# Sums of weights on VectorE behind the first operand sums, two transfer queues, and second-pass sums beside the last pair of the first pass

## The chip, the cores and the metric

One core of one Trainium2 chip runs the whole program in one launch. The metric is the device time in microseconds (us), given as the median over executions; every execution whose state is on record was in the undisturbed state ("fast", which means not more than 1.5% above the fastest of the same kernel), save one single look whose state can't be told. "Window" rows and "order of time" rows below count from the start of the profiled execution.

## The reference, cut to what matters

Two graph layers over 128 graphs of 64 nodes with 768 features, each behind a layer norm and a ReLU:

```python
h = jnp.maximum(_layernorm(x), 0.0)
x = x + layer0(h, adj, ...)    # three 768x768 products (Wadj, Wrev, Wself), two of them averaged
                               # over neighbours, and a relation table looked up by the entry of adj
h = jnp.maximum(_layernorm(x), 0.0)
x = x + layer1(h, adj, ...)    # six attention heads and a gate: two 768x768 products
```

The kernel makes one pass over all tiles for layer 0, then one for layer 1. A step of a pass handles two tiles of 128 rows, "a pair". The big products are computed blockwise with seven block products in place of eight; that needs four sums of weight blocks, called T1 to T4, and sums of the operands (S1 to S4). For layer 0 a sum of weights is three VectorE or GpSimd instructions (three matrices), for layer 1 two.

Of the kernel before, what the change touches and what calls it, by code (L numbers as in the profile page):

```python
# [8 lines left out]
F32 = mybir.dt.float32  # L9
# [6 lines left out]
P = 128  # L16
# [6 lines left out]
def kernel(  # L23
# [48 lines left out]
    nc = tc.nc  # L72
    G, N, D = x.shape
    NREL = e_t.shape[1]
# [9 lines left out]
    HALF = D // 2  # L84
# [25 lines left out]
    def row(v, parts):  # L110

        n = 1
        for s in v.shape:
            n *= s
        return bass.AP(tensor=v.tensor, offset=v.offset, ap=[[0, parts], [1, n]])
# [21 lines left out]
    for g in range(GT):  # L137
        s = slice(g * N, (g + 1) * N)
# [2 lines left out]
    mhalf = const.tile([P, 1], F32, name="mhalf")  # L141
    nc.vector.memset(mhalf, -0.5)

    def stats(src, to):

        st = small.tile([P, 2, 6], F32, name="st")
        for i in range(2):
            nc.vector.bn_stats(st[:, i, :], src[:, i * HALF : (i + 1) * HALF])
        mv = small.tile([P, 2], F32, name="mv")
        nc.vector.bn_aggr(mv, st.rearrange("p a b -> p (a b)"))  # L150
        ve = small.tile([P, 1], F32, name="ve")
        nc.vector.tensor_scalar(ve, mv[:, 1:2], EPS, None, op0=OP.add)
        nc.gpsimd.tensor_tensor(to[:, 0:1], ve, mhalf, op=OP.pow)
        nc.vector.scalar_tensor_tensor(to[:, 1:2], mv[:, 0:1], -1.0, to[:, 0:1],
                                       op0=OP.mult, op1=OP.mult)
# [3 lines left out]
    def block(name, mats, place):  # L159
        return [keep.tile([P, KH, HALF], F32, name=f"{name}{s}", tag=f"w{place}{s}") if s < 2 else  # L160
                keep.tile([P, KH, HALF], F32, name=f"{name}{s}", tag="wl", bufs=7)
                for s in range(mats)]

    def sums_of_weights(w, mats):


        for eng, to, a, b in ((nc.vector, "T1", "T3", "11"), (nc.vector, "T2", "22", "T1"),
                              (nc.gpsimd, "T3", "22", "T3"), (nc.vector, "T4", "21", "T2")):
            for s in range(mats):
                tc.keep_in_program_order(eng.tensor_sub(w[to][s], w[a][s], w[b][s]))  # L170


    bv, H1 = {}, {}

    def load_h(p):
        for k in range(2):
            t = 2 * p + k
            H1[t] = keep.tile([P, D], F32, name="h1", tag="x", bufs=8)
            nc.sync.dma_start(H1[t], H1D[p][k * P : (k + 1) * P, :])

    def fetch():

        def blk_of(name, place, h, q):
            bv[name] = block(f"bv{name}", 2, place)
            for s, src in enumerate((w_cat, hw_t)):
                nc.sync.dma_start(
                    bv[name][s],
                    src[h * HALF : (h + 1) * HALF, q * HALF : (q + 1) * HALF].rearrange(
                        "(k p) n -> p k n", p=P))

        def own(name, place):
            bv[name] = block(f"bv{name}", 2, place)

        return [(4, lambda: load_h(0)),
                (9, lambda: blk_of("11", "11", 0, 0)),
                (19, lambda: blk_of("21", "21", 1, 0)),
                (28, lambda: blk_of("T3", "T1", 0, 1)),
                (37, lambda: blk_of("22", "T2", 1, 1)),
                (47, lambda: own("T1", "T4")),
                (58, lambda: own("T2", "T3"))]  # L200


    with ExitStack() as px:
        wa = px.enter_context(tc.tile_pool(name="wa", bufs=1))
        work = px.enter_context(tc.tile_pool(name="work0", bufs=2))
# [3 lines left out]
        X, AI = {}, {}  # L209

        def load(p):
            if p >= NP:
                return
            AI[p] = work.tile([P, 2, 2, N], I32, name="ai")
            for d, src in ((0, adj), (1, adj_t)):
                nc.sync.dma_start(
                    AI[p][:, :, d, :],
                    src[p * 2 * GT : (p + 1) * 2 * GT].rearrange("(t g) i j -> (g i) t j", g=GT))
            for t in (2 * p, 2 * p + 1):
                X[t] = keep.tile([P, D], F32, name="x", bufs=8)  # L220
                nc.sync.dma_start(X[t], xf[t * P : (t + 1) * P, :])

        load(0)


        bw = {n: block(f"bw{n}", 3, n) for n in ("11", "21", "22", "T1", "T2", "T3", "T4")}

        def load_block(to, h, q):
            for s, src in enumerate((wadj_t, wrev_t, wself_t)):
                nc.sync.dma_start(  # L230
                    to[s], src.rearrange("(k h p) n -> h p k n", h=2, p=P)[h][:, :, q * HALF : (q + 1) * HALF])

        load_block(bw["11"], 0, 0)
        load_block(bw["21"], 1, 0)
        load_block(bw["T3"], 0, 1)
        load_block(bw["22"], 1, 1)
        et = wa.tile([P, NREL], F32, name="et")
        nc.sync.dma_start(et, e_t)
        wrt = work.tile([P, 2, D], F32, name="wrt", tag="a1")
        nc.sync.dma_start(wrt[:, 0, :], wr_t)  # L240
        nc.sync.dma_start(wrt[:, 1, :], wrr_t)

        bia = work.tile([5, D], F32, name="bia", tag="s3")
        for i, v in enumerate((br, brr, badj, brev, bself)):
            nc.sync.dma_start(bia[i : i + 1, :], row(v, 1))
        load(1)

        identb = wa.tile([P, P], BF16, name="identb")
        nc.vector.tensor_copy(identb, ident)
        blkb = wa.tile([P, P], BF16, name="blkb")  # L250
# [56 lines left out]

        def norm(t):
            to = small.tile([P, 2], F32, name="rn")
            stats(X[t], to)  # L310
            h = H0[t] = work.tile([P, D], F32, name="h0")
            nc.scalar.activation(h, X[t], AF.Relu, scale=to[:, 0:1], bias=to[:, 1:2])

        def prep(p):

            af = ADF[p] = work.tile([P, 2, 2, N], F32, name="af", bufs=1)
            nc.vector.tensor_copy(af, AI[p])
            ab = AB[p] = work.tile([P, 2, 2, N], BF16, name="ab", bufs=1)
            nc.vector.tensor_copy(ab, af)

# [33 lines left out]
        def count(p, k):  # L354

            eq = work.tile([P, 2, NG, N], BF16, name="eq", bufs=1)
            nc.vector.tensor_tensor(
                eq, GR[p][:, k, :, None, :].to_broadcast([P, 2, NG, N]),
                vals[:, None, :, :].to_broadcast([P, 2, NG, N]), op=OP.is_equal)
            nc.vector.tensor_tensor(  # L360
                eq, eq, WO[p][:, k, :, None, :].to_broadcast([P, 2, NG, N]), op=OP.mult)
            nc.vector.tensor_reduce(SUM[p][:, k], eq, AX.X, OP.add)
# [58 lines left out]
        def sum2(p):  # L421
            S2[p] = work.tile([P, KH, 3, P], F32, name="s2", bufs=1)
            for q in range(KH):
                nc.gpsimd.tensor_sub(S2[p][:, q], S1[p][:, q], A1[p][:, q, 0])  # L424

        def sum4(p):
            S4[p] = work.tile([P, KH, 3, P], F32, name="s4", bufs=1)
            for q in range(KH):
                nc.gpsimd.tensor_sub(S4[p][:, q], A1[p][:, q, 1], S2[p][:, q])
# [65 lines left out]
        def finish(p):  # L495
            for k in range(2):
                t = 2 * p + k
                to = small.tile([P, 2], F32, name="rn")
                stats(X[t], to)
                h = keep.tile([P, D], F32, name="hf", bufs=2)  # L500
                nc.scalar.activation(h, X[t], AF.Relu, scale=to[:, 0:1], bias=to[:, 1:2])
                nc.sync.dma_start(H1D[p][k * P : (k + 1) * P, :], h)
                nc.gpsimd.tensor_add(X[t], X[t], h)
                nc.sync.dma_start(XH1[p][k * P : (k + 1) * P, :], X[t])
# [23 lines left out]


        prep(0)  # L530
        norm(0)
        norm(1)
        prep_r(0)
# [1 line left out]
            for q in range(KH):  # L535
                operands(0, k, q)
        sum2(0)
        sums_of_weights(bw, 3)
        sum4(0)
        prep_c(0)  # L540
        late = [(14, build_table), (15, lambda: count(0, 0)),
# [9 lines left out]
    with ExitStack() as px:  # L551
        wb = px.enter_context(tc.tile_pool(name="wb", bufs=1))
        work = px.enter_context(tc.tile_pool(name="work1", bufs=2))
# [3 lines left out]
        XH, AI = {}, {}  # L557
# [231 lines left out]
        def before(p):  # L789

            if p >= NP:
                return []
            return [(0, lambda: load(p + 1)),
                    (11, lambda: turn(p, 0, 0)),
                    (14, lambda: turn(p, 0, 1)),
                    (17, lambda: turn(p, 1, 1)),
                    (20, lambda: turn(p, 1, 0))]
# [48 lines left out]
                steps.append((99, lambda q=q: final(t1, q * HALF, (q + 1) * HALF)))  # L846
            return steps

        bv["T4"] = block("bvT4", 2, "22")
        sums_of_weights(bv, 2)  # L850
        for _, step in before(0):
            step()
        for p in range(NP):
            more = [(3, lambda: finish(NP - 1))] if p == 0 else []
            if p == NP - 1:
                more += last()
            merged(main(p), before(p + 1) + behind(p - 1) + more)
# [45 lines left out]
```

## The kernel before: what the change touches

The sums of weights, T3 on GpSimd, all pinned in program order:

```python
def sums_of_weights(w, mats):
    for eng, to, a, b in ((nc.vector, "T1", "T3", "11"), (nc.vector, "T2", "22", "T1"),
                          (nc.gpsimd, "T3", "22", "T3"), (nc.vector, "T4", "21", "T2")):
        for s in range(mats):
            tc.keep_in_program_order(eng.tensor_sub(w[to][s], w[a][s], w[b][s]))
```

`keep_in_program_order` pins an instruction behind all that was written down before it for its engine; everything else may be moved by the scheduler. The transfers, all on one queue, in this order:

```python
load(0)                            # first pair: adjacency and x
load_block(bw["11"], 0, 0)         # four weight blocks, 1.77 MB each
load_block(bw["21"], 1, 0)
load_block(bw["T3"], 0, 1)
load_block(bw["22"], 1, 1)
nc.sync.dma_start(et, e_t)         # 40 KB, needed early by VectorE (es <- et, ids)
nc.sync.dma_start(wrt[:, 0, :], wr_t)
nc.sync.dma_start(wrt[:, 1, :], wrr_t)
# [cut: five bias rows]
load(1)                            # second pair
```

The opening of the first pass, and the start of the second:

```python
prep(0); norm(0); norm(1); prep_r(0)
for k in range(2):
    for q in range(KH):
        operands(0, k, q)          # first operand sums, from PSUM
sum2(0)
sums_of_weights(bw, 3)
sum4(0)
# [cut]
bv["T4"] = block("bvT4", 2, "22")  # second pass
sums_of_weights(bv, 2)
for _, step in before(0):
    step()                         # its first operand sums s3 and s1
```

## Time and profile before

| kernel before | us |
|---|---|
| median of three executions | 2695.43 (2694.94 to 2698.22) |
| profiled execution, first to last instruction (2700.46 as timed) | 2698.6 |
| TensorE busy / idle in it | 2628.7 / 69.9 |
| hole 1, wait for the first operand sums | 9.92, up to 27.95 |
| hole 2, wait for the second pair's converted adjacency | 8.08, up to 53.16 |
| hole 3, join of the passes, wait for `s1` | 8.97, up to 1587.29 |

TensorE is the engine that sets the time, so the table is read from its idle time: a change of order that shortens neither a hole nor the half clock behind one can't shorten the kernel. The prediction shows the lines themselves. A row in the order of time reads: start, length, engine and source line, operation, output<-input, shapes, number of instructions, and in brackets how long the engine stood before it and what released it.

### The profile page before, as it was taken

To read this page: it belongs to the slowest core of one execution; us is meant where nothing else is said; L and a number is where in the kernel's file an instruction comes from. 1 tells how busy PE (TensorE), PEld (TensorE's weight loads), DVE (VectorE), ACT (ScalarE), POOL (GpSimd) and SP (SyncE) were. 2 spreads that over 40 slices of the span, in tenths; PEclk is the share of its full clock that TensorE was granted. 3 is DMA by queue.
4 is the path that set the end of the run, shared out by engine and by line. 5 is a ranking of instruction groups with operands and counts; after the bars stand their busy time and mean duration, and the time that the engine had idled before them with its cause. 6 is when DMAs were issued, how large, how long until landed. Compare 5 with 4: busy or idle time off the path is not lost.

```text
span 2698.6 us, 29601 instructions
## 1 busy us (share of the span) xinstructions
PE 2628.7 (97%) x10348; PEld 1608.9 (60%) x10348; DVE 1814.8 (67%) x4235; ACT 843.3 (31%) x1892; POOL 632.1 (23%) x662
## 2 busy tenths in 40 slices
PE   5999999999999999999999989999999999999997
PEld 3556666565666656566665556666666666666664
DVE  6956465565646556564655258888888888888888
ACT  1212111121211112111111025555555555555555
POOL 3322232312223231222322231111111111111111
PEclk7999999999999999999999999999999999999998
DMA  5112121111212112121211322222222222222211
GB/s 172 45 38 74 38 75 37 53 60 38 74 38 75 38 45 67 37 75 38 74 37 42 135 79 73 72 66 68 69 70 73 73 68 67 70 69 73 73 60 47
DMA packets 91211, 173.47 MB, mean 64 GB/s; under 512 B 32958, under 2 KB 41521, under 8 KB 91062
## 3 DMA queue, kind: packets, MB, share of 16 engines
q1 hardware_dynamic: 91062, 171.58, 19.3%
q8 instruction: 82, 1.34, 0.2%
q14 instruction: 67, 0.55, 0.1%
HBM read 95.67 MB, written 75.50 MB: 63 GB/s over the span
## 4 chain that ended last, share of the span: by engine, by line
PE 71%; DVE 19%; ACT 6%; issue 3%; SPq 1%; DMA 1%; POOL 0%; ACTq 0%; DVEq 0%
PE pwa L443 20%; PE pwb L443 14%; PE pwd L443 7%; PE pwc L443 7%; PE pb L399 5%; PE pma L631 5%; PE pmc L631 5%; DVE no L712 4%; PE pmb L631 3%; DVE f L783 2%; ACT e L782 2%; DVE f L784 2%; DVE f L785 2%; DVE f L773 2%; PE ps L768 2%
## 5 line engine op out<-in xcount | busy, mean ns | idle before, releaser
L443 PE MATMUL pwa<-bwT,s 128*128 128x384 f32 x1152 | 391.2, 489 | 0.5 <-DVE x L460 0.5
L443 PEld LDWEIGHTS pwa<-bwT,s 128*128 128x128 f32 x1152 | 215.0, 190 | 145.6 <-issue 8.5
L631 PE MATMUL pma<-bvT,s 128*128 128x384 f32 x768 | 289.1, 487 | 0.0
L424 POOL TENSOR_TENSOR s<-s,a 128x384 f32<-128x384 f32 x96 | 94.8, 1014 | 633.1 <-PE pwa L443 596.7
L719 POOL TENSOR_TENSOR pr<-th,wsd 128x768 f32<-128x768 f32 x64 | 137.1, 2143 | 424.6 <-ACT th L708 217.5
L460 DVE TENSOR_TENSOR x<-pwa,x 128x384 f32<-128x384 f32 x128 | 69.5, 543 | 210.8 <-PE pwa L443 179.4
L443 PE MATMUL pwb<-bw,s 128*128 128x384 f32 x576 | 201.6, 489 | 0.0
L443 PE MATMUL pwb<-bwT,s 128*128 128x384 f32 x576 | 201.3, 495 | 0.0
L443 PE MATMUL pwa<-bw,a 128*128 128x384 f32 x576 | 197.5, 492 | 2.8 <-DVE x L460 2.8
L443 PE MATMUL pwd<-bwT,a 128*128 128x384 f32 x576 | 191.3, 486 | 0.0
L443 PE MATMUL pwc<-bw,a 128*128 128x384 f32 x576 | 191.0, 486 | 0.0
L411 ACT COPY a<-pb 128x768 f32<-128x768 f32 x96 | 73.7, 801 | 373.2 <-PE pb L399 373.2
L388 ACT COPY cntT<-pb 117x128 bf16<-117x128 bf16 (+1 forms) x128 | 27.8, 269 | 482.9 <-PE pb L386 482.9
L399 PE MATMUL pb<-r,h 64*128 64x192 f32 x1536 | 153.7, 339 | 18.2 <-DVE s L419 11.0
L399 PEld LDWEIGHTS pb<-r,h 64*128 64x128 f32 x1536 | 124.4, 189 | 73.6 <-issue 62.3
L717 ACT ACTIVATE dg<-idc,sd 128x64 f32<-128x64 f32 x384 | 128.5, 345 | 123.7 <-DVE no L712 123.5
L631 PEld LDWEIGHTS pma<-bvT,s 128*128 128x128 f32 x768 | 131.8, 191 | 53.3 <-issue 0.8
L712 DVE SCALAR_TENSOR_TENSOR no<-th,wsd 128x128 f32<-128x128 f32 x384 | 152.0, 396 | 5.5 <-ACT th L708 0.9
L631 PE MATMUL pmb<-bvT,s 128*128 128x384 f32 x384 | 146.6, 492 | 9.0 <-DVE s L616 9.0
L443 PEld LDWEIGHTS pwc<-bw,a 128*128 128x128 f32 x576 | 109.4, 190 | 76.3
L443 PEld LDWEIGHTS pwd<-bwT,a 128*128 128x128 f32 x576 | 109.4, 190 | 76.3 <-issue 0.2
L443 PEld LDWEIGHTS pwa<-bw,a 128*128 128x128 f32 x576 | 107.5, 192 | 73.7 <-issue 9.8
(141 smaller groups left out, 4618.0 us busy)
## 6 DMA issues: line engine op xcount, KB each, us to landing
x<-in_x_dram SPq DMA_DIRECT2D x64, 384.0 KB
h<-hf SPq DMA_DIRECT2D x64, 384.0 KB
xh<-x SPq DMA_DIRECT2D x64, 384.0 KB
h<-h SPq DMA_DIRECT2D x64, 384.0 KB
x<-xh SPq DMA_DIRECT2D x64, 384.0 KB
out_dram<-f SPq DMA_DIRECT2D x62, 384.0 KB
ai<-in_adj_dram SPq DMA_DIRECT2D x64, 64.0 KB
ai<-in_adj_t_dram SPq DMA_DIRECT2D x32, 64.0 KB
```

The source lines that it names most:

```text
L399: nc.tensor.matmul(ps[:, g, i * 3 * N : (i + 1) * 3 * N], H0[t][s, kb * P : (kb + 1) * P], rts[p % 2][s, k].rearrange("p s n -> p (s n)"), ...
L411: nc.scalar.copy(A1[p][:, q].rearrange("p h s (g n) -> p g (h s) n", g=GT), pv)
L424: nc.gpsimd.tensor_sub(S2[p][:, q], S1[p][:, q], A1[p][:, q, 0])
L443: nc.tensor.matmul(bank[b][:, :HALF], a()[:, q, s, :], bw[w][s][:, q, :], start=(first and q == s == 0), stop=(q == KH - 1 and s == 2), sk ...
L460: nc.vector.tensor_add(v, bank[b][:, :HALF], v)
L631: nc.tensor.matmul(bank[b, s][:, :HALF], a[p][:, q, :], bv[w][s][:, q, :], start=(first and q == 0), stop=(q == KH - 1), skip_group_check= ...
L712: nc.vector.scalar_tensor_tensor(no, th[:, h, :], 1.0, wsd[:, 1, h * DO : (h + 1) * DO], op0=OP.mult, op1=OP.mult, accum_out=sd[:, 1, h : ...
L717: nc.scalar.activation(dg[:, h, :], idc, AF.Copy, scale=sd[:, 1, h : h + 1])
L719: nc.gpsimd.tensor_mul(pr, th, wsd[:, 0, :].rearrange("p (h o) -> p h o", h=H))
L768: nc.tensor.matmul(po[:, i, :], PT[t][:, h, :], HS[t][:, h, :], start=True, stop=True)
L773: nc.vector.scalar_tensor_tensor(FF[t][:, h * DO : (h + 1) * DO], po[:, i, :DO], ri[:, i, :], bb, op0=OP.mult, op1=OP.add)
L782: nc.scalar.activation(e, f, AF.Exp, bias=mone)
```

## The change

The intent: no wait for a transfer on VectorE's path in the opening, no GpSimd sum beside VectorE's, and no sums left between the passes. Cut to its core:

```diff
-    def sums_of_weights(w, mats):                       # T3 on GpSimd
+    SUMS = {"T1": ("T3", "11"), "T2": ("22", "T1"), "T4": ("21", "T2"), "T3": ("22", "T3")}
+    def sum_of_weights(w, to, behind=False):            # all on VectorE
+        a, b = SUMS[to]
+        for s, t in enumerate(w[to]):
+            ins = nc.vector.tensor_sub(t, w[a][s], w[b][s])
+            if behind: tc.keep_in_program_order(ins)
     def stats(src, to, behind=False):
         for i in range(2):
-            nc.vector.bn_stats(st[:, i, :], ...)
+            ins = nc.vector.bn_stats(st[:, i, :], ...)
+            if behind and i == 0:                       # third pair's tiles only
+                tc.keep_in_program_order(ins)
         load(0)
+        nc.scalar.dma_start(et, e_t)                    # and the five bias rows
         load_block(bw["11"], 0, 0)
+        load(1)
         load_block(bw["21"], 1, 0)                      # T3, 22 as before
-        nc.sync.dma_start(et, e_t)
         # [cut: wrt as before; bias rows and load(1) no longer here]
# pins on the third pair's conversion and on counts of the first two pairs: [cut]
-        sums_of_weights(bw, 3)
+        for to in SUMS:
+            sum_of_weights(bw, to, behind=True)
# second pass: in the last pair of the first
-   (47, lambda: own("T1", "T4")),
-   (58, lambda: own("T2", "T3"))
+   (47, lambda: (own("T1", "T4"), sum_of_weights(bv, "T1"), sum_of_weights(bv, "T3"))),
+   (58, lambda: (own("T2", "T3"), sum_of_weights(bv, "T2")))
-        bv["T4"] = block("bvT4", 2, "22")
-        sums_of_weights(bv, 2)
         for _, step in before(0): step()
+        bv["T4"] = block("bvT4", 2, "22")
+        sum_of_weights(bv, "T4")
```

More of the change, by code (lines that the diff above doesn't have):

```diff
@@ L142, with stats @@
     nc.vector.memset(mhalf, -0.5)
-    def stats(src, to):
+    def stats(src, to, behind=False):
         st = small.tile([P, 2, 6], F32, name="st")
         for i in range(2):
-            nc.vector.bn_stats(st[:, i, :], src[:, i * HALF : (i + 1) * HALF])
+            ins = nc.vector.bn_stats(st[:, i, :], src[:, i * HALF : (i + 1) * HALF])
+            if behind and i == 0:
+                tc.keep_in_program_order(ins)
         mv = small.tile([P, 2], F32, name="mv")
@@ L162, in block @@
                 for s in range(mats)]
-    def sums_of_weights(w, mats):
-        for eng, to, a, b in ((nc.vector, "T1", "T3", "11"), (nc.vector, "T2", "22", "T1"),
-                              (nc.gpsimd, "T3", "22", "T3"), (nc.vector, "T4", "21", "T2")):
-            for s in range(mats):
-                tc.keep_in_program_order(eng.tensor_sub(w[to][s], w[a][s], w[b][s]))
+    SUMS = {"T1": ("T3", "11"), "T2": ("22", "T1"), "T4": ("21", "T2"), "T3": ("22", "T3")}
[3 more added lines that the diff above has]
+            ins = nc.vector.tensor_sub(t, w[a][s], w[b][s])
+            if behind:
+                tc.keep_in_program_order(ins)
     bv, H1 = {}, {}
@@ L198, in fetch @@
                 (37, lambda: blk_of("22", "T2", 1, 1)),
-                (47, lambda: own("T1", "T4")),
-                (58, lambda: own("T2", "T3"))]
+                (47, lambda: (own("T1", "T4"), sum_of_weights(bv, "T1"), sum_of_weights(bv, "T3"))),
+                (58, lambda: (own("T2", "T3"), sum_of_weights(bv, "T2")))]
     with ExitStack() as px:
@@ L223 @@
         load(0)
+        et = wa.tile([P, NREL], F32, name="et")
+        nc.scalar.dma_start(et, e_t)
+        bia = work.tile([5, D], F32, name="bia", tag="s3")
+        for i, v in enumerate((br, brr, badj, brev, bself)):
+            nc.scalar.dma_start(bia[i : i + 1, :], row(v, 1))
         bw = {n: block(f"bw{n}", 3, n) for n in ("11", "21", "22", "T1", "T2", "T3", "T4")}
@@ L236 @@
         load_block(bw["22"], 1, 1)
-        et = wa.tile([P, NREL], F32, name="et")
-        nc.sync.dma_start(et, e_t)
         wrt = work.tile([P, 2, D], F32, name="wrt", tag="a1")
@@ L241 @@
         nc.sync.dma_start(wrt[:, 1, :], wrr_t)
-        bia = work.tile([5, D], F32, name="bia", tag="s3")
-        for i, v in enumerate((br, brr, badj, brev, bself)):
-            nc.sync.dma_start(bia[i : i + 1, :], row(v, 1))
-        load(1)
         identb = wa.tile([P, P], BF16, name="identb")
@@ L309, in norm @@
             to = small.tile([P, 2], F32, name="rn")
-            stats(X[t], to)
+            stats(X[t], to, behind=(t // 2 == 2))
             h = H0[t] = work.tile([P, D], F32, name="h0")
@@ L316, in prep @@
             af = ADF[p] = work.tile([P, 2, 2, N], F32, name="af", bufs=1)
-            nc.vector.tensor_copy(af, AI[p])
+            ins = nc.vector.tensor_copy(af, AI[p])
+            if p == 2:
+                tc.keep_in_program_order(ins)
             ab = AB[p] = work.tile([P, 2, 2, N], BF16, name="ab", bufs=1)
@@ L356, in count @@
             eq = work.tile([P, 2, NG, N], BF16, name="eq", bufs=1)
-            nc.vector.tensor_tensor(
+            ins = nc.vector.tensor_tensor(
                 eq, GR[p][:, k, :, None, :].to_broadcast([P, 2, NG, N]),
                 vals[:, None, :, :].to_broadcast([P, 2, NG, N]), op=OP.is_equal)
+            if p < 2 and k == 0:
+                tc.keep_in_program_order(ins)
             nc.vector.tensor_tensor(
```

## The prediction

> **What bounds the kernel now.** I read the page's busy shares first, then a table of busy time by stretch, then the order of time in the two stretches that stand out, and last every instruction of the line that forms the sums of weights.
>
> ```profile
> PE 2628.7 (97%) x10348; PEld 1608.9 (60%) x10348; DVE 1814.8 (67%) x4235; ACT 843.3 (31%) x1892; POOL 632.1 (23%) x662
> ```
>
> TensorE is busy for 2628.7 of 2698.6 us, so only 69.9 us of idle time exist for any reordering to win back, plus what a lowered clock costs behind such a gap. The stretches show where they lie (columns: stretch, its length, busy time of each engine, granted clock, DMA share, GB/s):
>
> ```profile
> 0.00:10.00 10.00, 0.37 (x1) 0.10 (x1) 6.97 (x24) 1.28 (x1) 2.93 (x14) 1.00 0.76 247
> 10.00:20.00 10.00, 6.25 (x42) 4.84 (x42) 2.43 (x16) 5.28 (x7) 0.55 (x1) 1.00 1.06 377
> 20.00:30.00 10.00, 2.06 (x9) 1.65 (x10) 2.17 (x6) 0.37 (x1) 1.97 (x3) 0.58 0.83 282
> 40.00:50.00 10.00, 5.08 (x16) 2.66 (x14) 10.00 (x4) 0.00 (x0) 8.48 (x3) 0.94 0.00 0
> 50.00:60.00 10.00, 6.84 (x11) 2.18 (x11) 9.80 (x26) 2.05 (x2) 1.10 (x2) 0.50 0.06 13
> 60.00:70.00 10.00, 10.00 (x29) 4.87 (x30) 4.94 (x10) 1.59 (x2) 0.00 (x0) 0.70 0.00 0
> 1570.00:1580.00 10.00, 8.32 (x33) 4.68 (x31) 9.73 (x7) 3.44 (x6) 7.91 (x4) 1.00 0.94 330
> 1580.00:1590.00 10.00, 2.71 (x4) 1.51 (x5) 9.83 (x12) 0.00 (x0) 5.38 (x4) 0.57 0.38 144
> ```
>
> Three holes matter: 18 to 28 us, 45 to 53 us, 1578 to 1587 us. The rest of the idle time is the first 11.65 us (loads and first operands), 2.8 us at 100 to 102.65, and some 17 us in the drain from 2650 on; the change touches neither the first nor the last. In order of time:
>
> ```profile
> 26.56 0.31 DVE L273 TENSOR_TENSOR es<-et,ids 128x39 f32<-128x39 f32 x2 [13.60 <-DMA et<-in_e_t_dram]
> 27.95 1.65 PE L399 MATMUL pb<-r,h 64*128 64x192 f32 x8 [9.92 <-DVE s L419]
> 31.08 5.49 DVE L170 TENSOR_TENSOR bwT<-bwT,bw 128x1152 f32<-128x1152 f32 x3
> 36.49 15.75 DVE L170 TENSOR_TENSOR bwT<-bw,bwT 128x1152 f32<-128x1152 f32 x6
> 53.16 0.39 PE L347 MATMUL pb<-ab,blkb 128*128 128x256 bf16 x1 [8.08 <-DVE ab L319]
> 61.81 4.86 PE L443 MATMUL pwb<-bwT,s 128*128 128x384 f32 x8
> 102.65 7.77 PE L443 MATMUL pwa<-bw,a 128*128 128x384 f32 x18 [2.79 <-DVE x L460]
> 1587.29 4.21 PE L631 MATMUL pmb<-bvT,s 128*128 128x384 f32 x6 [8.97 <-DVE s L616]
> ```
>
> The first hole is VectorE standing for 13.60 us on `et`, a 40 KB table queued behind 8.0 MB; TensorE's operands wait behind it (9.92). The second: TensorE's in-order list reaches the second pair's row sums, whose input VectorE converts only after nine sums (31.08 to 52.24). The third: the same sums for the second pass, with TensorE needing the `s1` that follows them (8.97). The sums are slow because GpSimd forms T3 at the same time (duration in ns, least/median/most):
>
> ```profile
> L170 DVE TENSOR_TENSOR bwT<-bw,bwT x6: 1344/2951/3771, 36.5 to 50.9; 128x1152 f32<-128x1152 f32 x6
> L170 POOL TENSOR_TENSOR bwT<-bw,bwT x3: 3722/3732/3735, 37.4 to 44.8; 128x1152 f32<-128x1152 f32 x3
> ```
>
> **What the Trainium skill says.** (1) "GPSIMD Engine Reference", section 8, Key points: GpSimd shares its SBUF interfaces with VectorE and collides with VectorE instructions that have two SBUF inputs. The trace agrees: one sum takes 1.344 us alone and 3.771 us beside GpSimd's. (2) "TensorE: Matmul & The Clock Gate", Part 1: after an idle window of about 3.4 us the array runs at half clock, and needs about as long a busy one to recover. It agrees: after the 8.08 us gap the granted clock is 0.50, and 8 matmul instructions take 4.86 us against some 2.6 warm (18 take 5.8). (3) The same page, "Engine queue depths": VectorE is strictly first in, first out; the 13.60 us wait that held ready work shows it. (4) "DMA: Bandwidth & Descriptors", "Issuing engines are not separate DMA queues": transfers from several engines interleave on the same 16 DMA engines. A second queue therefore adds no bandwidth; it lets the small tables pass the big weights. The share of 1.06 at 377 GB/s says that bandwidth is the limit until 28 us.
>
> **The change part by part.** The built order of instructions says more than the diff: from the third pair to the end of the first pass, and in the second pass after its first pair, it is the same on every engine. So the 47.36 us of a pair stay, and only the opening and the join of the passes can move.
>
> *Transfers.* `et` and the five bias rows go to ScalarE's queue and land in the first few us: VectorE's 13.60 us wait goes. The second pair's load moves up behind the first weights (0.92 MB, about 2.4 us at 385 GB/s), landing near 13.5 us instead of 34.4.
>
> *VectorE's opening.* In the built order the second pair's conversion and statistics now stand before the first operand sums: about 20 instructions, 5.5 us from 13.3, with one wait on GpSimd's power: to 18.7. The first operand sums come at 18.8 to 19.9 (26.8 to 27.7 before); TensorE resumes at 20 after 2 us of idling, perhaps still warm, and runs to about 24 to 27. Then I see a flaw: only the first of two statistics instructions of a tile is pinned behind the sums. The second half of the third pair's first tile stands between the first and second operand sums. Its data come after all the weights, the second pair, 0.79 MB of relation weights and 0.13 MB of adjacency: `et` landed at 26.5 behind 8.0 MB; now 2.2 MB more stand ahead of or in it, 2.2/0.385 = 5.8 us, so 32.3 us. The operand sums then end at 34.7, not the 31.2 of before.
>
> *The twelve sums.* GpSimd's operand sums collide with the first three as before: 5.5 us. Nine more alone at 1.27 us from start to start (1.344 with its overlap): 11.4. 34.7 + 16.9 = 51.6 us, against 52.24 before without T3. As VectorE work this is even; what changes is what stands behind.
>
> *TensorE.* From the second operand sum at 33.9: row sums 0.4, three matmuls of two instructions cold at 1.3 = 3.9, five warm 3.2, the relation table 5.5 (8.7 cold before, about 4.4 warm), four 2.6, nine with T1 5.8: 55.3. The next operands need a reciprocal behind the sums, 51.6 + 3.9 of VectorE work = 55.5. From there a pair's rest at full clock: three blocks of 18 at 5.8 each and the last block 5.8 = 23.2, operand products 48 instructions 4.6, transposes and counts 2.8: 30.6, and 2 us of small waits: 88.1. VectorE's own remaining list of about 24 us ends near 80 to 83, because the third pair's preparation and counts are pinned away. So the second pair starts at 88 instead of 102.65, 14.5 earlier, and without the cold restart (7.77 against 5.8 for its first 18 instructions) another 1.9: 16.4. I take off 2.4 for a clock that may fall through the table's narrow matmuls and for waits at the end of the pair: 14.
>
> *The join of the passes.* T1 starts when the last pair's T4 matmuls are done (about 1553.5) and T3 follows, their transfers having stopped at 1553; T2 starts when T3's old block is free (about 1560). That is six sums, 8 us, in a stretch where VectorE is nearly empty. T4's two start at 1565.5 and end at 1568. Then `s3` and `s1` at 1569.5 to 1570.6, and TensorE needs `s1` at about 1572.9, so no wait: 8.97 us gone, plus half of the 4.21 us cold stretch, 2.1. One risk is an addition into x that now stands behind T2 and must free a bank before 1563.4: it comes at 1562.5. I take 10.5 of 11.1.
>
> Sum: 2695.4 - 14 - 10.5 = 2671 us.
>
> **The rivals.** *A: the misplaced statistics cancel the opening's gain.* TensorE idles from about 26 to 34 and is cold again; if the table stays cold (+4) and VectorE's counts still end last (the chain of waits before goes through them between 67 and 102), the opening gives 5 to 8: about 2678. For it: the hole only moves. Against it: the 8 us gap at 45 and its 13 us of half clock have no cause left. *B: the load is hidden and the opening as the author meant it.* If the third pair's tile lands by 26, the sums end near 44 and the opening gives 22: about 2662. Against it: 1.06 of DMA share. *C: the join stalls anew.* If the late addition or the old blocks hold a sum, TensorE waits 2 to 5 us and the clock may drop: 2675. *D: the second pass takes the gain back.* VectorE is at 80% there, but TensorE is at 99% (39.7 of 40 us), so an earlier start should reach the end whole.
>
> **Range and chances.** The opening alone spreads from 6 to 22, the join from 6 to 11.5, and the day's runs spread by 3.3 us: 2662 to 2681. Over 2% would need 54 us, nearly all idle time there is; over 2% slower would need something that no step here makes. So 0.01 faster, 0.985 same, 0.005 slower.
>
> **What would show it.** VectorE's wait on `et` gone; a wait of about 11 us on the transfer of x ahead of a statistics instruction, ending near 32; L173 sums of 1.34 us with none on GpSimd; the first matmul of the second pair (18 instructions into `pwa`) near 88; in the join no TensorE gap over 1 us and a granted clock of 1.00 from 1540 on. I am wrong if the sums stay near 2.5 us beside an idle GpSimd, if TensorE idles over 4 us between 34 and 88, if the join keeps a wait on `s1`, or if the distance between two pairs leaves 47.4.

## The result, and the profile after

The changed kernel takes 2676.58 us (2676.50 to 2677.65, 4 executions) against 2696.82 us (2694.94 to 2700.03, 4 executions) of the kernel before beside it: ratio 0.9925, 95% interval 0.9907 to 0.9942, so faster, but by less than 2%. Ratios here are the mean time of one kernel's fast executions over that of the other's of the same rounds, so not quite the ratio of the medians quoted. By medians 20.2 us are gained, where 24.4 (2695.43 to 2671) were predicted.

The busy line of the changed kernel's page:

```profile
PE 2620.3 (98%) x10348; PEld 1607.3 (60%) x10348; DVE 1810.1 (68%) x4240; ACT 843.2 (32%) x1892; POOL 612.6 (23%) x657
```

TensorE's idle time fell from 69.9 to 54.4 us, and its busy time by 8.4 us with the same 10348 instructions; the mean granted clock rose from 0.990 to 0.995, so less of it ran at half clock. The second queue moves 0.06 MB. By stretch, as before:

```profile
20.00:30.00 10.00, 4.34 (x18) 2.47 (x18) 0.49 (x2) 1.40 (x2) 2.00 (x2) 0.91 1.07 372
30.00:40.00 10.00, 6.19 (x13) 3.53 (x14) 7.73 (x8) 0.00 (x0) 5.95 (x4) 0.57 0.47 156
40.00:50.00 10.00, 10.00 (x30) 4.71 (x29) 10.00 (x9) 0.00 (x0) 1.09 (x1) 1.00 0.00 0
100.00:110.00 10.00, 9.20 (x50) 5.79 (x50) 10.00 (x17) 4.15 (x6) 5.57 (x4) 1.00 0.47 165
1570.00:1580.00 10.00, 10.00 (x34) 6.03 (x33) 3.63 (x7) 0.48 (x1) 1.99 (x2) 1.00 0.32 119
```

The first hole is still there, moved to 25 to 34 us: VectorE is busy for 0.49 us of 20 to 30, while transfers run at 372 GB/s. The second hole is gone (40 to 50: TensorE 10.00 at clock 1.00), the third too (1570 to 1580). VectorE has no idle time left at 100 to 110 (it was busy for 9.64 of 10 before). VectorE's work in order of time, the three rows that set the opening:

```profile
32.27 0.56 DVE L148 BATCH_NORM_STATS2 st<-x 128x6 f32<-128x384 f32 x1 [11.78 <-DMA x<-in_x_dram]
34.59 5.65 DVE L173 TENSOR_TENSOR bwT<-bwT,bw 128x1152 f32<-128x1152 f32 x3
40.16 12.29 DVE L173 TENSOR_TENSOR bwT<-bw,bwT 128x1152 f32<-128x1152 f32 x9
```

The wait for `et` is gone, and in its place VectorE stands 11.78 us on the transfer of a tile of x: the half of the third pair's statistics that the change did not pin, with operand sums behind it. The nine sums without a GpSimd partner take 12.29 us, 1.37 each. TensorE's rows (`pb<-r,h` are operand products; `pwa`, `pwb`, `pwc` the main accumulations; `wrt,es` the relation table):

```profile
20.64 0.92 PE L407 MATMUL pb<-r,h 64*128 64x192 f32 x8 [1.36 <-DVE s L427]
33.81 0.40 PE L353 MATMUL pb<-ab,blkb 128*128 128x256 bf16 x1 [8.83 <-DVE s L427]
34.00 4.05 PE L451 MATMUL pwa<-bw,a 128*128 128x384 f32 x6
41.41 1.45 PE L295 MATMUL pb<-wrt,es 128*81 128x384 f32 x4
56.25 0.92 PE L407 MATMUL pb<-r,h 64*128 64x192 f32 x8 [1.76 <-DVE r L358]
89.86 4.03 PE L451 MATMUL pwa<-bw,a 128*128 128x384 f32 x12
102.55 1.57 PE L407 MATMUL pb<-r,h 64*128 64x192 f32 x16 [0.80 <-DVE r L358]
1559.98 2.10 PE L641 MATMUL pmb<-bvT,s 128*128 128x384 f32 x6
```

Before, the matmuls behind the second hole ran at half clock to about 66 us. Now the clock is half at 34 us (six instructions in 4.05 us, which take 2.10 warm) and back by 41.4 (four table instructions in 1.45 us, 2.77 in the profile before). The second pair starts at 89.86 instead of 102.65, without a cold restart. The last row is the first use of the second pass's T1: no wait, full clock, where it was 4.21 us behind a wait of 8.97.

From the third pair's second block to the last pair's fourth, the two traces run in step: 157.61 to 1548.59 before, 144.84 to 1535.82 after, 1390.98 us in both. The two ends are where the time moved: 12.8 us in the opening, and 11.6 in the join (a later product of the second pass, 1603.09 before, 1578.72 after: 24.4 in all).

### The profile page after: what moved, and what is told of

It reads as the page before. It is cut to its first block, busy times and chain, and to the rows that moved or that the text cites. A ratio compares the mean times of both kernels' runs of the same rounds, so it can differ in the third digit from the quotient of the medians.

```text
span 2674.7 us, 29599 instructions
## 1 busy us (share of the span) xinstructions
PE 2620.3 (98%) x10348; PEld 1607.3 (60%) x10348; DVE 1810.1 (68%) x4240; ACT 843.2 (32%) x1892; POOL 612.6 (23%) x657
## 3 DMA queue, kind: packets, MB, share of 16 engines
q8 instruction: 82, 1.34, 0.2%
## 4 chain that ended last, share of the span: by engine, by line
PE 71%; DVE 19%; ACT 6%; issue 3%; DMA 1%; SPq 0%; POOL 0%; ACTq 0%; DVEq 0%
PE pwa L451 20%; PE pwb L451 14%; PE pwd L451 7%; PE pwc L451 7%; PE pma L641 5%; PE pb L407 5%; PE pmc L641 5%; DVE no L722 4%; PE pmb L641 3%; DVE f L793 2%; ACT e L792 2%; DVE f L794 2%; DVE f L795 2%; DVE f L783 2%; PE ps L778 2%
## 5 line engine op out<-in xcount | busy, mean ns | idle before, releaser
L451 PEld LDWEIGHTS pwb<-bwT,s 128*128 128x128 f32 x576 | 106.2, 190 | 69.0 <-issue 6.7
```

Source lines behind the costliest of these rows:

```text
L451: nc.tensor.matmul(bank[b][:, :HALF], a()[:, q, s, :], bw[w][s][:, q, :], start=(first and q == s == 0), stop=(q == KH - 1 and s == 2), sk ...
```

## The experiments

Each kernel was correct. "Beside" means in the same rounds on the same chip. The changed kernel ran again beside experiments 2 and 3 only. Where experiments 5, 7, 8 and 9 are set against it, or against `pin_both`, the runs are of other rounds, those of 7, 8 and 9 also of other chips; the kernel before had medians of 2695.89 to 2698.91 in the four sets of rounds, so a difference of some 3 us between sets needs a trace to back it.

### 1. The changed kernel once more (`after_again`)

No edit; a check of the result in other rounds.

> The changed kernel once more, as a yardstick on the same chip as the next three. Expected 2676.6 us, within 1.5, and again a wait of VectorE of about 11.8 us on the transfer of x ahead of a statistics instruction, ending near 32.3 us.

Measured: 2676.78 us (2676.65 to 2678.61, 4 executions), ratio to the kernel before 0.9923 (0.9909 to 0.9936). The kernel before, beside it, had 2698.91 us and spread over 2694.42 to 2700.33. VectorE's wait on x was there again (11.65 us, up to 32.37). The changed kernel repeats within about 2 us, the kernel before only within 6; that spread comes up again in experiment 6.

### 2. Both halves of the statistics pinned (`pin_both`)

```diff
-            if behind and i == 0:
+            if behind:
```

In the built order a single VectorE instruction moves: the second half of the third pair's first statistics, from between the operand sums to behind the twelve sums.

> One instruction moves: the second statistics instruction of the third pair's first tile goes behind the sums of weights too. My theory: its 11.8 us wait holds the second and third operand sums and with them everything on VectorE, so without it the operand sums end near 23 us, the twelve sums wait for the last weights (landing near 29 us) and end near 43 instead of 52.4; TensorE is then held by the relation table's transfers until about 35 us. About 8 us less than the changed kernel: 2668, between 2665 and 2671. Rival: the wait only covers another one (weights and the table come at the same time, or VectorE's list behind the sums ends last whatever stands ahead), then 2674 to 2677.

Measured: 2668.14 us (2667.55 to 2670.24, 4 executions), ratio 0.9888 (0.9873 to 0.9903), beside the changed kernel's 2676.78: another 8.6 us for one condition. VectorE's sums, then two TensorE rows:

```profile
23.45 5.99 DVE L173 TENSOR_TENSOR bwT<-bwT,bw 128x1152 f32<-128x1152 f32 x3
29.36 12.29 DVE L173 TENSOR_TENSOR bwT<-bw,bwT 128x1152 f32<-128x1152 f32 x9
```

```profile
33.91 0.84 PE L297 MATMUL pb<-bia,eb 5*81 5x384 f32 x2 [1.97 <-DMA eb<-ebr]
80.08 4.03 PE L451 MATMUL pwa<-bw,a 128*128 128x384 f32 x12
```

The sums start 11.1 us earlier (23.45, not 34.59), the second pair 9.8 earlier (80.08, not 89.86); 8.1 of these are left at the third pair, as the second pair now takes 56.69 us from its start to the third's second block, against 54.98. The traced execution was the longest of its four (2670.24) and loses 1.9 us again between the join and the end, where the granted clock was 0.83 at 2630 to 2640 us (1.00 in the changed kernel). So the misplaced statistics cost what the prediction feared: the rest of rival B's gain. A smaller new hole shows: the table's bias matmul waits for `eb`, two tiny transfers that are queued behind the third pair's tiles.

### 3. The opening alone, and the join alone (`opening_only`, `join_only`)

The first is the changed kernel with the second pass's sums put back:

```diff
-   (47, lambda: (own("T1", "T4"), sum_of_weights(bv, "T1"), sum_of_weights(bv, "T3"))),
-   (58, lambda: (own("T2", "T3"), sum_of_weights(bv, "T2")))
+   (47, lambda: own("T1", "T4")),
+   (58, lambda: own("T2", "T3"))
+        bv["T4"] = block("bvT4", 2, "22")
+        sums_of_weights(bv, 2)          # as before, T3 on GpSimd
         for _, step in before(0): step()
-        bv["T4"] = block("bvT4", 2, "22")
-        sum_of_weights(bv, "T4")
```

> The changed kernel with the second pass's sums put back as before (all behind the first pass, T3 on GpSimd). If opening and join add up, as the two traces say (12.8 and 11.6 us), this loses the 11.6 us: 2688, between 2686.5 and 2690, with TensorE's wait of about 9 us on s at the join back. Rival: the second pass, where VectorE is busy 80%, swallows part of a gain at the join, then 2680 to 2685.

The second is the kernel before with exactly these lines the other way round.

> The kernel before with the join's part alone. Additive: 2696.8 - 11.6 = 2685, between 2683 and 2687; no TensorE gap over 1 us at the join. Rival (the opening's gain is the larger one in unprofiled runs and the join's is partly swallowed): 2688 to 2692.

Measured beside each other: `opening_only` 2688.65 us (2687.72 to 2689.11, 5 executions), ratio 0.9965 (0.9952 to 0.9977); `join_only` 2684.69 us (2683.84 to 2689.97, 5 executions), ratio 0.9955 (0.9943 to 0.9968). The first use of the second pass's T1, in `opening_only` and then in `join_only`:

```profile
1574.45 3.75 PE L647 MATMUL pmb<-bvT,s 128*128 128x384 f32 x6 [8.84 <-DVE s L632]
```

```profile
1567.86 2.10 PE L638 MATMUL pmb<-bvT,s 128*128 128x384 f32 x6
```

The wait of 8.84 us and the cold group are there without the join part and gone with it. The join is worth 2688.65 - 2676.78 = 11.9 us on top of the opening; the opening 2684.69 - 2676.78 = 7.9 on top of the join, 2698.91 - 2688.65 = 10.3 by itself. The two don't differ clear of noise: by means they are 8.8 and 9.4 (and the join 11.3 on top of the opening, 12.0 by itself), since the kernel before and `join_only` both spread over 6 us.

### 4. One table on the other queue (`et_only`)

The kernel before with one line changed; all four sums, their engines and all other loads stay:

```diff
-        nc.sync.dma_start(et, e_t)
+        nc.scalar.dma_start(et, e_t)
```

> The kernel before with one line changed: the table `et` goes to ScalarE's queue. Theory 1, that wait was most of the opening: VectorE forms the first operand sums some 11 us earlier, then waits for the weight blocks themselves (T3's block about 21.5, 22's about 26 us), the first three sums end at 27 and the other six, still beside GpSimd, at about 42.7 instead of 52.24 us. The second hole moves up by 9.6 us with everything behind it: the second pair starts at 93 instead of 102.65, and the time is about 2687 us (2684 to 2690). Rival 2, the whole bundle is needed (the nine sums beside GpSimd hold TensorE as long as before, only earlier idle turns into later idle): 2693 or more.

Measured: 2687.31 us (2684.75 to 2690.74, 5 executions) against 2695.89 (2693.13 to 2700.00, 9 executions), ratio 0.9967 (0.9955 to 0.9980). VectorE's six sums, then TensorE:

```profile
26.96 15.74 DVE L170 TENSOR_TENSOR bwT<-bw,bwT 128x1152 f32<-128x1152 f32 x6
```

```profile
43.63 0.40 PE L347 MATMUL pb<-ab,blkb 128*128 128x256 bf16 x1 [9.67 <-DVE ab L319]
88.29 6.07 PE L443 MATMUL pwa<-bw,a 128*128 128x384 f32 x18 [2.79 <-DVE x L460]
```

Theory 1 holds: the six sums end at 42.7, still slowed by GpSimd, and the second hole comes at 43.6 instead of 53.2 with its length unchanged. The second pair starts even earlier than expected, at 88.29 and not 93, and less half clock followed (the table's second four matmuls took 1.52 us, 2.85 in the first profile). So 8.6 us of the kernel hung on where one 40 KB transfer stood in a queue, about as much as the whole new opening brought (7.9 to 10.3 in experiment 3).

### 5. That table and the join, nothing else (`et_join`)

`join_only` with the one-line edit of experiment 4.

> The kernel before with two things alone: the table `et` on ScalarE's queue, and the second pass's sums beside the first pass's last pair. If the two gains add up, 8.6 us (the run with `et` alone against its kernel before) and 11.9 us (the join, from the run with the opening alone) make 2675.5 us (2674 to 2678), so as much as the whole change, and the rest of its opening (twelve sums on VectorE, second pair ahead, pins) was worth nothing net while the statistics stood in the wrong place. If the rest of the opening carried a share of its own, this version is slower than the changed kernel's 2676.7 by that share: 2680 or more.

Measured: 2676.75 us (2675.06 to 2679.02, 5 executions), ratio 0.9922 (0.9908 to 0.9936). The changed kernel had 2676.78 us and 0.9923 in experiment 1. The gains add, and two small parts of the change give the time of the whole. The remaining parts (twelve sums on VectorE, the second pair's load and preparation ahead, the pins) brought nothing net while the statistics stood in the wrong place. `pin_both`, which has them with the statistics put right, is 8.6 us below this version (2668.14): that is what they are worth together. Single parts among them are tested in experiments 7 and 8 only.

The kernel is not the same inside, though. In this execution:

```profile
90.52 7.76 PE L450 MATMUL pwa<-bw,a 128*128 128x384 f32 x18 [2.79 <-DVE x L467]
```

The gap of 2.79 us ahead of the second pair is still there, and here it was followed by half clock (7.76 us for 18 instructions, 6.07 after the same gap in experiment 4). The changed kernel has neither, and its executions spread less.

### 6. Where the kernel before spreads (`before_again`)

The kernel before with nothing but a line break added, one look (2696.17 us, span 2694.4, against 2698.6 of the first profile).

> The kernel before, one more look, for its spread of 6 us between executions. If the spread comes from how long the half clock lasts behind its gaps of 8 us, the trace differs from the first one's only in the length of the matmul groups behind the gaps at 53, 102 and 1587 us (8 instructions into `pwb` 4.86 us there, the first 18 of the second pair 7.77, the first 6 of the second pass's T1 4.21), not in any wait by more than 0.5 us, and the span by the sum of these differences. If transfers make it, the waits on DMA before 30 us differ by as much.

```profile
52.82 0.40 PE L347 MATMUL pb<-ab,blkb 128*128 128x256 bf16 x1 [7.08 <-DVE ab L319]
61.17 2.85 PE L443 MATMUL pwb<-bwT,s 128*128 128x384 f32 x8
99.99 6.07 PE L443 MATMUL pwa<-bw,a 128*128 128x384 f32 x18 [2.79 <-DVE x L460]
```

The first row starts 0.34 us earlier than in the first profile, though waits here did differ by more than the expected 0.5 us: 7.08 against 8.08 in this row, and 8.59 against 9.92 in the first hole. Behind it the same eight instructions take 2.85 us where they took 4.86, and behind an equal gap of 2.79 us the 18 take 6.07 where they took 7.77: 2.0 and 1.7 us of half clock, which with the 0.34 and 0.3 in the table matmuls, less 0.2 further on, make the 4.2 us by which this span is shorter. Between these two executions the difference is thus the length of the half clock behind the holes of the opening; at the join they agree (waits of 8.98 and 8.97). That the whole spread of 6 us has this cause is not shown by two traces. The profile that the prediction used was of a long execution (2700.46 us timed, above all 3 of its timed runs), so its opening was 4.2 us longer than the one seen here.

### 7. T3 back on GpSimd in the opening (`t3_gpsimd`)

```diff
-            ins = nc.vector.tensor_sub(t, w[a][s], w[b][s])
+            eng = nc.gpsimd if behind and to == "T3" else nc.vector
+            ins = eng.tensor_sub(t, w[a][s], w[b][s])
```

> The changed kernel with the first pass's T3 back on GpSimd, the rest as it is: nine sums on VectorE, of which six lie beside GpSimd's three. Collision theory: the six take 15.75 us as before (2.6 us each) instead of the 12.29 of nine alone, so VectorE is free at 55.9 instead of 52.4 us, TensorE's next operands at 59.8: about 2680 us (2678 to 2682). Rival, GpSimd's sums are free help (three fewer on VectorE, 1.37 us each): VectorE free at 48.3, and the time falls to 2674 to 2676, as the wait of 1.76 us on the reciprocal goes.

Measured: 2683.83 us (2683.64 to 2684.11, 5 executions), ratio 0.9953 (0.9939 to 0.9966), 7 us slower than the changed kernel. VectorE's six sums, then TensorE:

```profile
39.82 15.74 DVE L174 TENSOR_TENSOR bwT<-bw,bwT 128x1152 f32<-128x1152 f32 x6
```

```profile
59.35 1.65 PE L408 MATMUL pb<-r,h 64*128 64x192 f32 x8 [10.03 <-DVE r L359]
```

Six sums beside GpSimd's three take 15.74 us, nine alone 12.29: GpSimd's help costs VectorE 3.4 us more than doing the work itself, as expected. The pace shows in single sums of the kernel before: the three that lay wholly beside GpSimd's took 3.76 to 3.77 us each, GpSimd's own 3.72 to 3.74, and VectorE's last two, with GpSimd done, 1.34. So VectorE got one sum done for each of GpSimd's. The time is worse than expected because the scheduler also moved things: in the built order of this kernel the second pair's operand products stand in front of twelve of T1's eighteen matmuls, so TensorE has nothing left to do and waits 10.03 us, then runs cold. The 3.4 us are shown; how the 7 us of time divide between the two causes is not separated by this run.

### 8. Without the pins that put work off (`no_defer`)

```diff
-            if p == 2: tc.keep_in_program_order(ins)              # third pair's conversion
-            if p < 2 and k == 0: tc.keep_in_program_order(ins)    # counts
```

> The changed kernel without its three pins that put off the counts and the third pair's conversion; the sums and the statistics stay pinned. In its built order three instructions of the first pair's counts (3.9 us) stand ahead of the first operand sums, so fill part of the 11.8 us for which VectorE waits for x, and the third pair's conversion stands among the sums' followers instead of behind the second pair's start. My theory: the pins only move VectorE's load to 100 to 117 us, where TensorE waits 2.9 us for it; without them those waits shrink by some 2 us: about 2674.5 us (2672 to 2677). The author's reason, that unpinned work gets in the way of the sums: 2679 to 2684, with TensorE waiting between 52 and 88 us for more than the 4.1 us it waits in the changed kernel.

Measured: 2680.66 us (2680.04 to 2681.15, 5 executions), ratio 0.9941 (0.9928 to 0.9953). My theory fell: it is 3.9 us slower than the changed kernel of experiment 1 (other rounds, another chip; no run of one lies in the range of the other), not 2 faster. TensorE:

```profile
22.71 1.65 PE L403 MATMUL pb<-r,h 64*128 64x192 f32 x8 [4.72 <-DVE s L423]
90.03 0.43 PE L390 MATMUL pb<-identb,c 128*117 128x128 bf16 x2 [2.92 <-ACT cntT L392]
94.38 4.03 PE L447 MATMUL pwa<-bw,a 128*128 128x384 f32 x12
```

The counts put themselves ahead of the first operand sums (a wait of 4.72 where the changed kernel has 1.36), a new wait of 2.92 us comes at the end of the first pair, and the second pair starts at 94.38, 4.5 us later. The part that I had in mind is there too, but smaller: from the second pair's start to the third's second block it takes 53.27 us instead of 54.98. The pins cost 1.7 us there and save 4.5 ahead of it. The time lies in the range given for the author's reason, but its sign did not show as written: between 52 and 88 us TensorE idles for 3.55 us here and 4.10 in the changed kernel; the loss is a mean clock of 0.91 there, and the wait that ends at 90.

### 9. Three attempts at a faster version (`pin_eb_wrt`, `best_c`, `best_d`)

All start from `pin_both`. The first removes the small hole at 31 to 34 us:

```diff
+        nc.sync.dma_start(wrt[:, 0, :], wr_t)          # moved ahead of block 22
+        nc.sync.dma_start(wrt[:, 1, :], wrr_t)
         load_block(bw["22"], 1, 1)
-            nc.sync.dma_start(eb[1:2, :], ebr)         # and eb[2:5]
+            nc.scalar.dma_start(eb[1:2, :], ebr)
```

> The version with both statistics halves pinned, and besides the two tiny transfers of `eb` on ScalarE's queue and the relation weights ahead of the last weight block. In the version with both pinned, TensorE idled 2.2 us between 31.5 and 33.9 us (0.23 on the relation weights, 1.97 on `eb`) and the relation table behind it ran half cold, some 2 us longer. Theory 1, the reciprocal then holds: TensorE would reach the second pair's operand products at about 43 us, but their reciprocal stands behind the twelve sums on VectorE (41.6 us) and is ready at 45.4, so of 4.2 us only 1.8 are kept: about 2666.3 us (2665 to 2667.5). Rival 2, nothing holds it: 2664. Rival 3, VectorE's list at 93 to 117 us takes it all: 2668. A wait of about 2 us ahead of the first operand products of the second pair, with VectorE's `r` as releaser, would show theory 1.

Measured: 2667.50 us (2667.39 to 2669.64, 4 executions), ratio 0.9894 (0.9880 to 0.9907).

```profile
46.33 0.92 PE L407 MATMUL pb<-r,h 64*128 64x192 f32 x8 [1.86 <-DVE r L358]
60.32 0.92 PE L407 MATMUL pb<-r,h 64*128 64x192 f32 x8 [0.33 <-DVE s L427]
80.05 4.03 PE L451 MATMUL pwa<-bw,a 128*128 128x384 f32 x12
```

The hole is gone and the expected wait for the reciprocal stands at 46.33 in its place. But nothing was kept. A stretch of half clock followed (24 products in 3.47 us; in `pin_both` they took 2.74), and even so TensorE came early to the next product that needs VectorE, at 60.32 us, where it had waited 1.07 us up to 60.35 in `pin_both`. VectorE has that operand sum at the same time in both, so the second pair starts at 80.05, as it did at 80.08. The time, at the upper edge of theory 1's range and 0.5 us from rival 3's 2668, does not separate the two.

The second puts the reciprocal's chain between the sums T1 and T2:

```diff
-        for to in SUMS:
-            sum_of_weights(bw, to, behind=True)
+        sum_of_weights(bw, "T1", behind=True)
+        late += [(7 + i, lambda to=to: sum_of_weights(bw, to, behind=True))
+                 for i, to in enumerate(("T2", "T4", "T3"))]
```

> As the run before it, but the second pair's reciprocal stands between the sums T1 and T2 on VectorE. If the reciprocal was what held TensorE, its products start with no wait at about 43 us and the second pair starts about 4.2 us earlier than in the version with both statistics pinned (80.08 us there): about 2664 us (2662.5 to 2665.5). If VectorE's list at 93 to 117 us decides (10.00 of 10 busy there), the waits in that stretch grow by what is won and the time stays at 2666 to 2668.

Measured: 2668.41 us (2666.90 to 2668.80, 4 executions), ratio 0.9894 (0.9881 to 0.9908). The wait for the reciprocal is gone, and the next one takes its place:

```profile
49.01 0.92 PE L407 MATMUL pb<-r,h 64*128 64x192 f32 x8 [1.73 <-ACT tv L300]
78.83 4.03 PE L451 MATMUL pwa<-bw,a 128*128 128x384 f32 x12
```

The second pair starts 1.2 us earlier, not 4.2; the median does not show it, and lies just outside both ranges. ScalarE's copy waited for a buffer that VectorE's counts held, so the third gives it another:

```diff
-            v = work.tile([P, D], F32, name="tv", tag="eq", bufs=1)
+            v = keep.tile([P, D], F32, name="tv", tag="hf", bufs=2)
```

> As the version with the reciprocal between the sums (2668.4), where TensorE waited 1.73 us (2.6 in all behind the group before) at 49 us for ScalarE's copy of the relation table's PSUM bank: that copy goes into a buffer that shares its place with the counts' product `eq`, so waits for VectorE's counts. Here it has a place that is free. If that wait was the one that took the gain, the second pair starts near 76 us (78.83 there) and the time falls to about 2665.5 us (2664 to 2667). If VectorE's list up to 117 us holds TensorE in any case, the waits between 90 and 117 us grow from 3.9 us and the time stays at 2667 to 2668.5.

Measured: 2669.44 us (2667.80 to 2670.17, 4 executions), ratio 0.9896 (0.9881 to 0.9912).

```profile
57.54 1.65 PE L407 MATMUL pb<-r,h 64*128 64x192 f32 x8 [3.13 <-DVE s L427]
```

Neither expectation held: the copy's wait went and TensorE arrived at the next product 3.9 us earlier (54.41, after 58.28), but VectorE had the operand sums only 1.6 us earlier, so TensorE stood 3.13 us for them (0.82 in the version ahead), and the next 18 matmuls took 8.30 us instead of 6; the second pair starts at 80.86. From 30 to 60 us VectorE was busy for 29.9 of 30 us in this trace. In these three trials, what TensorE wins by one wait less it spends at the next product of VectorE. The four versions with both statistics pinned lie within 2 us of each other, all faster than both kernels; the one-condition edit of experiment 2 is the one to take. A version beyond it would have to take work off VectorE in this stretch; none was tried.

## Why the prediction was right or wrong

**The total.** 2671 was predicted, 2676.6 measured, inside 2662 to 2681 and within 2%, so the range and the class held. The gain fell 4.2 us short (20.2, not 24.4), and the kernel before measured 1.4 higher beside it, which makes the 5.6 us. Trace against trace, though, the two gains are 12.8 (14 taken) and 11.6 (10.5 taken): 24.4 in all, where the prediction took 24.5. That the two errors cancel is luck. The step that was mis-sized is the base: gains read in a profiled execution that took 2700.46 us were subtracted from a median of 2695.43. This is 5.0 of the 5.6 us; another 0.5 is lost behind the join (1095.5 us from 1603.09 to the end before, 1096.0 from 1578.72 after).

**The join: right, term by term.** Taken at 10.5 of 11.1 worked out; 11.6 in the traces, 11.9 by experiment 3. Shifting by the 12.8 us of the opening, T1 was expected at 1540.7 and starts at 1540.5; T4's two at 1552.7 and run from 1552.8; and no wait at `s1`: the longest TensorE gap there is 0.30 us, at a granted clock of 1.00. Rival C fell with this. Rival D fell too: behind the join the second pass took 0.5 us longer, so it kept nearly all of the gain.

**The wait that replaces the one removed: right.** "32.3 us" for the third pair's half tile measured 32.27; operand sums "end at 34.7", 34.6; VectorE's twelve sums "51.6", 52.4 as the nine took 1.37 each and not 1.27 from start to start. TensorE's next operands "55.5", 56.25. Experiment 2 confirms the flaw by its removal, and its cost: 8.6 us, where rival B had put 9.

**The clock behind the first hole: mostly right.** It did fall (0.57 at 30 to 40), but was back for the relation table, which took 4.4 us (41.41 to 45.83) and not 5.5, so rival A's extra 4 us did not come; nor did VectorE's counts end last, for VectorE waited 5.91 us for TensorE up to 89.07. By its number alone rival A (2678) came closer than the prediction, with a mechanism that the trace does not show.

**The opening's size: one term failed, and the ground was a long execution.** "So the second pair starts at 88" measured 89.86: the operands came 0.75 us late and the rest took 33.6 us, not 32.6. "And without the cold restart (7.77 against 5.8 for its first 18 instructions) another 1.9" failed. The cold restart did go, but from the second pair's start to the third pair's second block it takes 54.98 us after and 54.96 before. From the second pair's second block to the third's VectorE, with the work that the pins put off, is now busy for 41.1 of 49.06 us (28.7 of 47.36 before); TensorE waits 0.80 us for `r` and 0.57 for `s` there and is busy 0.34 longer, 1.7 in all, which is what the cold start had cost. I had asked what the pins free between 52 and 88 us, not what they load at 100. The 2.4 us held back covered most of this, so 14 became 12.8. By medians the opening measured less, 10.3 alone and 7.9 next to the join. The likely cause is the ground that the sum stood on. I took 102.65 and 7.77 from the one profiled execution as the kernel's; another of the same kernel shows 99.99 and 6.07 (experiment 6). In 2.7 + 1.7 = 4.4 us the sum counted half clock that this other execution does not have: against it the opening gains 8.6 us (144.84 against 153.44).

**Its own signs of being wrong.** Two of four were touched, both by little: TensorE idles for 4.10 us between 34 and 88 us ("over 4"), and the second pair is 49.06 us from the third where it was 47.36. The sums at 1.37 us and the join without a wait came as said.

**Readings that were off.** Point (2) says that the trace agrees. It does for the loss of clock, but not for the recovery: TensorE had no gap over 0.3 us from 53.16 us on, and the clock was still half up to about 66. Point (4) has bandwidth as the limit until 28 us; the DMA share falls from 1.07 at 24 to 26 us to 0.52 at 26 to 28. The drain from 2650 on has 18.2 us of idle TensorE, not 17, and 8.5 us of small waits in the second pass before it are not listed. None of these carries the sum.

**What the bundle hid.** The prediction gave each part a cost but not each part's share alone. Experiments 4 and 5 do: the transfer of `et` and the join together give the measured gain, and the sums of weights, which the title names first, with the second pair's load and the pins, add none until the statistics are pinned.

## What to carry to other kernels

When a pin is used to order work, pin the whole group: one unpinned instruction that waits for a transfer holds all that stands behind it on its engine (11.78 us on VectorE here), and here it hid 8.6 us of the change's value. Before rewriting an opening, look for the smallest transfer that a critical engine waits for and try moving only that. And take two profiles of the kernel before, and subtract a gain read in a trace from the time of the execution that was traced: here a gap of TensorE cost its length plus a stretch of half clock, and that stretch differed by 4 us between two executions of one kernel.

## What the Trainium skill lacked or had wrong

- "DMA: Bandwidth & Descriptors", section "Issuing engines are not separate DMA queues", says that issuing on several engines will only save the time that it takes to initiate a transfer. Here it saved more. In the kernel before, SyncE issued the 40 KB table at 16.76 us and it landed only at 26.56, behind the weights of the same queue; with nothing but this table on ScalarE's queue (issued at 0.73 us), VectorE first used it at 12.34 us without a wait, and the kernel became 8.6 us faster (ratio 0.9967).
- "TensorE: Matmul & The Clock Gate", Part 1, gives about one busy window of 3.4 us to recover and, as the window runs freely, a first stretch that varies. The runs agree that it varies, but behind a gap of 7 to 8 us half clock lasted from 53.16 to about 66 us in one execution and from 52.82 to about 61 in another, under the relation table's matmuls of 81 and 5 rows. Behind equal gaps of 2.79 us, shorter than that window, it came twice (7.77 and 7.76 us for 18 instructions) and three times not (6.07).
